# Two graph attention layers on one core: row sums, bias rows and a scatter of layer 0 in another place

## The chip, the cores and the metric

The kernel runs on one core of a Trainium2 chip. The metric is the device time of one execution in microseconds (us); less is better. The engines are named as in the profile: PE is TensorE, DVE is VectorE, ACT is ScalarE, POOL is GpSimd, SP is SyncE.

## The reference

Two layers of attention over a graph of 2708 nodes with 1024 features. Row i of the matrix `adj` holds ones at the neighbours of node i. Biases and weights are inputs; all is float32.

```
# layer 0
f = x @ Wf + bf ;  g = x @ Wg + bg
e = relu(f @ g.T)
attention = softmax(where(adj > 0, e, NEG), axis=1)
x = layernorm(x + attention @ (x @ W + bW))
# layer 1
h = x @ W1 ;  e = leaky_relu(h @ a1 + (h @ a2).T, 0.2)
attention = softmax(where(adj > 0, e, NEG), axis=1)
x = layernorm(x + relu(attention @ h))
```

`layernorm` takes mean and variance over the 1024 features of a row.

## The kernel before, in words

**Stages.** A node has few neighbours (at most 40), so the kernel never forms the 2708 x 2708 scores. It first reads `adj`, finds each row's neighbours as lists, and multiplies weights together (`M` = Wf times the transpose of Wg), so that a score is a dot product of `x M` of one node, plus a constant row, with the raw `x` of a neighbour. Then comes layer 0, block after block, and then layer 1. A last part (`general_path`) runs only for inputs whose lists don't fit, which is not the case here.

**Blocks and tiles.** Nodes are sorted by the number of neighbours and cut into groups of 32; four groups make a block of 128 nodes, and there are 22 blocks, one of them a small one. For a group, neighbours are gathered as tiles of 128 rows: 32 nodes times four neighbours. A group with up to 4t neighbours has t tiles, and a block of layer 0 some 20. The tiles of the gathered `x` rows live in `ring`, which has 20 places, so one block's tiles fill it. `u.tiles` puts the tiles of groups 0 and 1 first, by t, and then those of groups 2 and 3; gathers are issued in that order (line 635).

**A turn of layer 0's loop** (its body is around line 1039), for block `b`, the one before it (`back`) and the one after (`nxt`):

1. `sums` (line 703) multiplies the softmax weights `u.st` (128x32 for each tile) with the tiles in `ring` and adds them in the PSUM tile `po`. A tile has two matmuls, one for each half of the 1024 features. TensorE's columns are used as four column tiles of 32, told by `place`: column tile c takes group c in the first half of the features and group (c + 2) mod 4 in the second. Four matmuls, one for each column tile, make a step.
2. When both halves of a tile are done, its place in `ring` is free, and `gathers` (line 660) issues the gathers of the next block into free places, on POOL's queue.
3. The row sums of the softmax, `u.rs`, are added over the partitions by small matmuls with `stack` into a PSUM tile `pt`; their reciprocal `ri` scales `po` when ACT copies it to `y`.
4. TensorE turns the next blocks' `x` (`x_turn`), multiplies the sums of the block before with `W` (`product` with the bias bW), the `x` of a later block with `M` (`f_product`, with the constant row), and turns `y` for the next turn of the loop.
5. ACT spreads `x M` over 128 partitions (`Fr`), DVE takes the dots of it with the gathered tiles (`dots`), and the softmax (`soft`) makes the next block's `u.st`, and last its `u.rs` (line 701).
6. `close(back)` (line 919) is a generator: it adds the residual `z` and takes the layernorm's statistics; then ACT scales `z` and SP stores it to `X1S`; then DVE takes two dots that layer 1 needs, into further columns of `z`; last, POOL scatters `z` to the table `T1` in DRAM, which layer 1 gathers from. It is begun at the end of a turn of the loop (line 1080) and continued in the next one. `z` is a single buffer, `zs`, for all blocks but the last two; `load_residual` (line 913) fills it by a gather on POOL's queue.

**Bias rows.** A bias row of float32 values is held as three rows of bfloat16 that add up to it: `rows3[0:3]` for the constant row of `x M`, `rows3[32:35]` for bW. A matmul of `ones3` (three rows of ones) with them begins each product's accumulation (lines 546 and 566).

**What sets the order.** Each engine runs its instructions in program order: `InOrder` (line 61) pins it, and Tile puts in the semaphores that the data needs. So the order of calls in the loop is the order in each engine's queue. On POOL, after the tile gathers of `sums`, the turn of the loop issues `load_x` (`xb`, a later block's own rows), `load_residual` (`z`), and four list gathers of `load_lists` (`SL`). The PSUM pools `ps_t` and `ps_m` have two buffers each, `ps_s` (for `po`) has one.

Of the kernel before, what the change touches and what calls it, by code (L numbers as in the profile page):

```python
# [8 lines left out]
F32 = mybir.dt.float32  # L9
BF16 = mybir.dt.bfloat16  # L10
# [96 lines left out]
def listed_path(ctx, tc, x, adj, Wf, bf, Wg, bg, W, bW, W1, a1, a2, out):  # L107

    nc = tc.nc
    P = 128  # L110
# [36 lines left out]
    make_identity(nc, ident)  # L147
    ones = const.tile([P, 1], F32, name="ones")
    nc.gpsimd.memset(ones, 1.0)
    ones3 = const.tile([35, P], BF16, name="ones3")  # L150
    nc.gpsimd.memset(ones3, 1.0)

    stack = const.tile([P, 32], F32, name="stack")
    rep = const.tile([P, Q, 32], F32, name="rep")
# [16 lines left out]
    f1 = const.tile([P, NB], F32, name="f1")  # L171
    nc.gpsimd.memset(f1, 0.0)
    s0 = const.tile([P, 1], F32, name="s0")
    rows3 = const.tile([35, D], BF16, name="rows3")
    c3, b3 = rows3[0:3], rows3[32:35]
    scores = [const.tile([P, Q, QT], F32, name=f"scores{i}") for i in range(2)]
    for t in scores:
# [357 lines left out]
    def product(n, xT, w, row=None):  # L535


        pm = ps_m.tile([P, H, 512], F32, name="pm")
        for h in range(H):
            half_product(pm, h, n, xT, w, row)  # L540
        return pm

    def half_product(pm, h, n, xT, w, row=None):
        c = slice(h * 512, (h + 1) * 512)
        if row is not None:
            pe.matmul(pm[:n, h, :], ones3[row:row + 3, :n], rows3[row:row + 3, c], start=True, stop=False)
        for k in range(KC):
            pe.matmul(pm[:n, h, :], xT[:, k, :n], w[:, k, c],
                      start=(row is None and k == 0), stop=(k == KC - 1))

    def two_products(n, xT, w, row=None):

        halves = [ps_m.tile([P, H, 512], F32, name="pm") for h in range(H)]
        for h in range(H):
            half_product(halves[h], h, n, xT, w, row)
        return halves

    def split_product(xT, w, parts, row=None, pm=None):

        pm = ps_m.tile([P, H, 512], F32, name="pm") if pm is None else pm
        for h in range(H):
            c = slice(h * 512, (h + 1) * 512)
            if row is not None:
                pe.matmul(pm[:32, h, :], ones3[row:row + 3, :32], rows3[row:row + 3, c], start=True, stop=False)
            for k in range(KC // Q):
                for p in range(Q):
                    i = p * KC // Q + k
                    pe.matmul(pm[32 * p:32 * p + 32, h, :], xT[:, i, :32], w[:, i, c],  # L570
                              start=(k == 0 and (row is None or p > 0)), stop=(k + 1 == KC // Q))
        yield
        act.copy(parts, flat(pm))
        yield
        pm = ps_m.tile([P, H, 512], F32, name="pm")
        for h in range(H):
            pe.matmul(pm[:, h, :], rep, parts[:, h * 512:(h + 1) * 512], start=True, stop=True)
        return pm
# [63 lines left out]
    class Layer:  # L642
# [57 lines left out]
            u.rs = small.tile([P, Q], F32, name="rs")  # L700
            dve.tensor_reduce(u.rs[:, :u.G], sc, AX.X, ALU.add)

        def sums(self, u, po, hooks, y):

            pt = ps_t.tile([P, 4, P], F32, name="pt")
            place = lambda k, h: 32 * ((k + 2 * h) % 4)
            for h in range(H):  # L710
                for k in range(u.G):
                    j = place(k, h)
                    pe.matmul(pt[j:j + 32, 0, h:h + 1], stack, u.rs[:, k:k + 1], start=True, stop=True)
            ri = small.tile([P, H], F32, name="ri")
            spans = [(slice(0, P), slice(0, H))] if u.G == 4 else \
                [(slice(j, j + 32), slice(h, h + 1)) for h in range(H) for j in (place(0, h),)]
            for rows, h in spans:
                dve.reciprocal(ri[rows, h], pt[rows, 0, h])
            index = {(k, t): m for m, (k, g, t) in enumerate(u.tiles)}

            queues = []
            for c in range(4):
                two = [(k, h) for h, k in enumerate((c, (c + 2) % 4)) if k < u.G]
                queues.append([(k, h, t) for t in range(u.T) for k, h in two if t < TILES[u.gs[k]]])
            done, halves = 0, {}
            while any(queues):
                now = [q.pop(0) for q in queues if q]
                for k, h, t in now:
                    j = place(k, h)
                    pe.matmul(po[j:j + 32, h, :], u.st[:, u.col[k, t], :],  # L730
                              self.rows(u.at + index[k, t])[:, h * 512:(h + 1) * 512],
                              start=(t == 0), stop=(t == TILES[u.gs[k]] - 1))
                for k, h, t in now:
                    halves[k, t] = halves.get((k, t), 0) + 1
                    if halves[k, t] == H:
                        self.free.add(u.at + index[k, t])
                        self.gathers()
                        for f in hooks.get(done, []):
                            f()
                        done += 1  # L740
            for k, fs in sorted(hooks.items()):
                if k >= done:
                    for f in fs:
                        f()
            for h in range(H):
                rows = slice(0, P) if u.G == 4 else slice(place(0, h), place(0, h) + 32)
                c = slice(h * 512, (h + 1) * 512)
                act.activation(y[rows, c], po[rows, h, :], AF.Copy, scale=ri[rows, h:h + 1])
# [107 lines left out]
    with ExitStack() as s0s:  # L856
# [155 lines left out]
        for k, u in enumerate(units):  # L1012
            nxt = units[k + 1] if k + 1 < len(units) else None
            b = u.b
            back = seq[k - 1] if k > 0 else None
            ahead = seq[k + 2] if k + 2 < NB else None

            first = k == 0
            po = ps_s.tile([P, H, 512], F32, name="po")
            y[b] = yp.tile([P, D], F32, name="y")  # L1020
            if back is not None:
                for _ in yTs[back][1]:
                    pass
            reps = list(range(len(nxt.gs))) if nxt is not None and not first else []
            for r in reps[:1]:
                replicate(nxt.b, r)
            next(closing, None)
            if loaded is not None:
                q_dot(loaded)
                loaded = None  # L1030
            next(closing, None)
            for r in reps[1:3]:
                replicate(nxt.b, r)
            if nxt is None:

                for _ in closing:
                    pass
                Wp[back] = product(P, yTs.pop(back)[0], Wt, 32)
            lay.sums(u, po, {12: [lambda s=closing: [None for _ in s]]}, y[b])
            closing = iter(())  # L1040
            if ahead is not None and not first:
                x_turn(ahead)
            if k + 3 < NB and not first:
                loaded = seq[k + 3]
                load_x(loaded)
            if back is not None and nxt is not None:
                load_residual(back)
                if back > 0:
                    Wp[back] = product(P, yTs.pop(back)[0], Wt, 32)
                else:  # L1050
                    Wp[back] = whole(split_product(yTs.pop(back)[0], Wt, frp.tile([P, D], F32, name="Fr"), 32))
            if k + 2 == NB:
                load_residual(b)
            spreading = iter(())
            if ahead is not None and not first:
                spreading = q_spread(ahead)
                next(spreading)
            for r in reps[3:]:
                replicate(nxt.b, r)
            if ahead is not None and not first:  # L1060
                f_product(ahead)
            if ahead == NB - 1:
                sp.dma_start(M, W1.rearrange("(k p) d -> p k d", p=P))
            yT = tp.tile([P, KC, P], F32, name="xT")
            steps = turn(y[b], nrows[b], yT, halves=True)
            next(steps)
            yTs[b] = yT, steps
            if k + 2 == NB:
                for _ in steps:
                    pass  # L1070
            if k + 4 < NB and not first:
                load_lists(seq[k + 4])
            if nxt is not None:
                dots(nxt, 0, len(nxt.tiles))
            for _ in spreading:
                pass
            if nxt is not None:
                soft(nxt)
            if back is not None:
                closing = close(back)  # L1080
                next(closing)
        b = NB - 1
        load_residual(b)
        for _ in yTs[b][1]:
            pass
        Wp[b] = two_products(P, yTs.pop(b)[0], Wt, 32)
        for _ in closing:
            pass
        for _ in close(b):
# [521 lines left out]
```

## Time and profile before

| | us |
|---|---|
| median of 3 runs | 1772.31 |
| lowest, highest | 1768.69, 1783.73 |
| the profiled execution | 1778.06 |
| its span | 1776.3 |
| gathers of `ring` from `x`: 405 on POOL, busy | 438.6 |
| dots of layer 0: 402 on DVE, busy | 494.4 |
| matmuls into `po` from `ring`, both layers: 2616, busy | 322.7 |
| bias matmuls into `pm`: 86, busy | 33.7 |
| idle of PE ahead of the row sums (340 small matmuls) | 27.3 |

The lists and the weights take the first 276 us of the span, layer 0's loop the time to 1172 us, with a start of its first sums at 276.86 us, and layer 1 the rest. Each engine's instructions are shown with the idle time ahead of them and what ended it. Busy times of one engine don't add up to a bound: an engine can be busy in one stage and wait in another, and what counts is the wait that ends last in each turn of the loop.

### The profile page before, as it was taken

Reading aid. Unit: us, or ns where it says so; the run is one execution under the profiler, and the core shown is the slowest. Engines: PE = TensorE matmul, PEld = TensorE weight load, DVE = VectorE, ACT = ScalarE, POOL = GpSimd, SP = SyncE. Lnnn points to the kernel's source line nnn. Section 1 sums busy time; section 2 is a strip of 40 time slices with the busy share of each in tenths; the row PEclk is TensorE's granted clock in tenths of the full one; section 3 lists DMA queues with packets and bytes.
Section 4 is the critical chain, followed back from the end, with each engine's and each line's share of the span. In section 5 each row is a group of like instructions: output and inputs, shape, how many; then the busy total and the mean of one; then the engine's idle time right before and its main releaser. Section 6 shows DMA issues by size and latency. Waiting matters only on the chain. (4 is left out here: it accounts for less than half of the span.)

```text
span 1776.3 us, 22882 instructions
## 1 busy us (share of the span) xinstructions
PE 1586.4 (89%) x6969; PEld 677.2 (38%) x6969; DVE 1295.3 (73%) x4262; ACT 643.4 (36%) x902; POOL 1188.0 (67%) x1192
## 2 busy tenths in 40 slices
PE   5999389899999999999999999739899897998896
PEld 3444133343444443443444444313344333343342
DVE  5879756888888888888888887637656556665652
ACT  4545454444444455454555554101111111111111
POOL 8878476467666666667666664167777777777740
PEclk9999789899999999999999999969999999999998
DMA  7646168568777777777787787299999999999960
GB/s 284 245 160 240 44 227 318 207 213 289 291 283 270 264 250 256 272 282 266 277 295 278 268 296 297 88 359 368 365 369 394 392 392 378 383 395 391 391 250 37
DMA packets 149984, 502.79 MB, mean 283 GB/s; under 512 B 32340, under 2 KB 32372, under 8 KB 147144
## 3 DMA queue, kind: packets, MB, share of 16 engines
q0 software_dynamic: 132032, 428.29, 65.3%
q1 hardware_dynamic: 10202, 55.72, 8.4%
q10 hardware_dynamic: 7618, 17.23, 2.7%
q8 instruction: 57, 0.93, 0.2%
q14 instruction: 75, 0.61, 0.1%
HBM read 509.64 MB, written 33.75 MB: 306 GB/s over the span
## 5 line engine op out<-in xcount | busy, mean ns | idle before, releaser
L71 POOL DMA_INDIRECT ring<-in_x_dram,SL x405 | 438.6, 1083 | 253.1 <-issue 91.4
L71 DVE SCALAR_TENSOR_TENSOR j<-ring,Fr 128x1024 bf16<-128x1024 f32 x402 | 494.4, 1230 | 82.5 <-DMA ring<-in_x_dram,SL 55.7
L71 PE MATMUL po<-ring,st 128*32 128x512 f32 x2616 | 322.7, 618 | 47.8 <-ACT y L71 30.4
L71 ACT COPY Fr<-pm 32x1024 f32<-32x1024 f32 (+2 forms) x353 | 340.7, 965 | 21.1 <-PE pm L71 16.4
L71 PE MATMUL pm<-M,yT 128*128 128x512 f32 (+1 forms) x704 | 313.3, 598 | 0.5 <-ACT yT L71 0.5
L71 PE MATMUL pm<-M,xT 128*128 128x512 f32 x672 | 307.2, 611 | 0.0
L71 PE MATMUL pm<-Wt,xT 128*128 128x512 f32 (+1 forms) x704 | 303.5, 599 | 0.0
L71 POOL DMA_INDIRECT ring<-T,SL x249 | 246.9, 992 | 83.3 <-issue 69.9
L71 ACT ACTIVATE scores<-scores 128x12 f32<-128x12 f32 (+9 forms) x65 | 14.0, 216 | 669.3 <-DVE scores L71 669.3
L71 PEld LDWEIGHTS pm<-M,yT 128*128 128x128 f32 (+1 forms) x704 | 127.8, 186 | 184.7 <-issue 183.5
L71 PEld LDWEIGHTS pm<-M,xT 128*128 128x128 f32 x672 | 127.1, 194 | 165.3 <-issue 165.3
L71 PEld LDWEIGHTS po<-ring,st 128*32 128x32 f32 x2616 | 103.8, 114 | 222.9 <-issue 182.3
L71 POOL DMA_INDIRECT more<-T,SL x156 | 154.7, 992 | 47.5 <-issue 40.7
L71 PEld LDWEIGHTS pm<-Wt,xT 128*128 128x128 f32 (+1 forms) x704 | 125.0, 186 | 151.8 <-issue 151.1
L409 POOL TENSOR_TENSOR adj<-adj,iota 128x2708 f32<-128x2708 f32 (+3 forms) x23 | 130.5, 5685 | 24.4 <-ACT adj L71 24.3
L412 DVE MAX8 cand<-adj 128x8 f32<-128x136 f32 (+2 forms) x440 | 97.2, 285 | 35.8 <-POOL adj L409 35.8
L71 PE MATMUL pm<-halfT,WfT 128*128 128x512 f32 x256 | 113.2, 597 | 1.1 <-ACT WfT L71 1.1
L71 POOL DMA_INDIRECT SL<-LD,idq x85 | 86.0, 1011 | 25.8 <-issue 22.4
L71 PE MATMUL po<-more,st 128*32 128x512 f32 x624 | 83.8, 632 | 17.8 <-ACT y L71 17.8
L71 DVE TENSOR_SCALAR scores<-ring,f1q 128x4 f32<-128x4 f32 (+6 forms) x69 | 16.0, 238 | 99.3 <-DMA ring<-T,SL 95.9
L71 PEld LDWEIGHTS pm<-halfT,WfT 128*128 128x128 f32 x256 | 48.0, 192 | 57.4 <-issue 54.7
L71 ACT ACTIVATE y<-po,ri 128x512 f32<-128x512 f32 (+1 forms) x88 | 57.5, 678 | 20.9 <-PE po L71 20.3
(211 smaller groups left out, 1509.0 us busy)
## 6 DMA issues: line engine op xcount, KB each, us to landing
adj<-in_adj_dram SPq DMA_DIRECT2D x21, 1354.0 KB
X1S<-z SPq DMA_DIRECT2D x19, 512.0 KB
ring<-in_x_dram,SL POOLq DMA_INDIRECT x405, 6.6
rows<-in_L_gnn_Wg_dram ACTq DMA_DIRECT2D x8, 512.0 KB
rows<-in_L_gnn_Wf_dram ACTq DMA_DIRECT2D x8, 512.0 KB
rows<-in_L_gnn_W_dram ACTq DMA_DIRECT2D x8, 512.0 KB
Wt<-in_L_gnn_W_dram ACTq DMA_DIRECT2D x1, 4096.0 KB
M<-in_L_gnn_W_dram SPq DMA_DIRECT2D x1, 4096.0 KB
```

Source lines behind the costliest of these rows:

```text
L71: made = self.tc.keep_in_program_order(op(*args, **kwargs))
L409: nc.gpsimd.tensor_tensor(k[:n, cut], k[:n, cut], iota[:n, cut], op=ALU.mult)
L412: nc.vector.max(cand[:n, s, :], k[:n, s * SEG:min((s + 1) * SEG, N)])
```

## The change

In `sums`, the row sums' small matmuls move from ahead of the first tile's matmuls to behind the step after which four tiles (or `u.T`, if less) are done; the reciprocal is emitted behind the last tile's matmuls. Column tiles 2 and 3 begin with the second half of the features instead of the first. The hook that ran the rest of `close(back)`, its scatter, when 12 tiles were done is gone: the loop runs that rest when `sums` has returned, with all its gathers issued. `ones3` becomes `pick`, 128 rows with two columns, one for each bias; `rows3` has 128 rows, zero but for the two times three; the bias matmul contracts over all 128 rows. In `product` and `two_products` both halves' bias matmuls now come ahead of both halves' other matmuls.

```diff
-    ones3 = const.tile([35, P], BF16, name="ones3")
-    nc.gpsimd.memset(ones3, 1.0)
+    pick = const.tile([P, 2], BF16, name="pick")
+    nc.gpsimd.memset(pick, 0.0)
+    nc.gpsimd.memset(pick[0:3, 0:1], 1.0)
+    nc.gpsimd.memset(pick[32:35, 1:2], 1.0)
...
-    rows3 = const.tile([35, D], BF16, name="rows3")
+    rows3 = const.tile([P, D], BF16, name="rows3")
+    nc.gpsimd.memset(rows3, 0.0)
...
         for h in range(H):
+            bias_row(pm, h, n, row)
+        for h in range(H):
             half_product(pm, h, n, xT, w, row)
...
+    def bias_row(pm, h, n, row):
+        pe.matmul(pm[:n, h, :], pick[:, row:row + 1].to_broadcast([P, n]), rows3[:, h * 512:(h + 1) * 512], start=True, stop=False)
+
     def half_product(pm, h, n, xT, w, row=None):
         c = slice(h * 512, (h + 1) * 512)
-        if row is not None:
-            pe.matmul(pm[:n, h, :], ones3[row:row + 3, :n], rows3[row:row + 3, c], start=True, stop=False)
...
-        def sums(self, u, po, hooks, y):
+        def sums(self, u, po, y):
...
-            pt = ps_t.tile([P, 4, P], F32, name="pt")
             place = lambda k, h: 32 * ((k + 2 * h) % 4)
-            for h in range(H):
-                for k in range(u.G):
-                    j = place(k, h)
-                    pe.matmul(pt[j:j + 32, 0, h:h + 1], stack, u.rs[:, k:k + 1], start=True, stop=True)
-            ri = small.tile([P, H], F32, name="ri")
...
+            def totals():
+                pt = ps_t.tile([P, 4, P], F32, name="pt")
+                for h in range(H):
+                    for k in range(u.G):
+                        j = place(k, h)
+                        pe.matmul(pt[j:j + 32, 0, h:h + 1], stack, u.rs[:, k:k + 1], start=True, stop=True)
+                return pt
...
                 two = [(k, h) for h, k in enumerate((c, (c + 2) % 4)) if k < u.G]
+                if c > 1:
+                    two.reverse()
...
             while any(queues):
+                if pt is None and done >= min(4, u.T):
+                    pt = totals()
...
                         self.gathers()
-                        for f in hooks.get(done, []):
-                            f()
                         done += 1
...
+            if pt is None:
+                pt = totals()
+            ri = small.tile([P, H], F32, name="ri")
...
-            lay.sums(u, po, {12: [lambda s=closing: [None for _ in s]]}, y[b])
+            lay.sums(u, po, y[b])
+            for _ in closing:
+                pass
```

The bias matmul of `split_product` changes in the same way, and the calls pass the column 1 of `pick` instead of the row 32.

More of the change, by code (lines that the diff above doesn't have):

```diff
@@ L553, in two_products @@
         halves = [ps_m.tile([P, H, 512], F32, name="pm") for h in range(H)]
+        if row is not None:
+            for h in range(H):
+                bias_row(halves[h], h, n, row)
         for h in range(H):
@@ L565, in split_product @@
             if row is not None:
-                pe.matmul(pm[:32, h, :], ones3[row:row + 3, :32], rows3[row:row + 3, c], start=True, stop=False)
+                pe.matmul(pm[:32, h, :], pick[:, row:row + 1].to_broadcast([P, 32]), rows3[:, c], start=True, stop=False)
             for k in range(KC // Q):
@@ L701, in soft @@
             dve.tensor_reduce(u.rs[:, :u.G], sc, AX.X, ALU.add)
-        def sums(self, u, po, hooks, y):
-            pt = ps_t.tile([P, 4, P], F32, name="pt")
+        def sums(self, u, po, y):
             place = lambda k, h: 32 * ((k + 2 * h) % 4)
-            for h in range(H):
-                for k in range(u.G):
-                    j = place(k, h)
-                    pe.matmul(pt[j:j + 32, 0, h:h + 1], stack, u.rs[:, k:k + 1], start=True, stop=True)
-            ri = small.tile([P, H], F32, name="ri")
[L715 to L718, printed above, removed]
+            def totals():
+                pt = ps_t.tile([P, 4, P], F32, name="pt")
+                for h in range(H):
+                    for k in range(u.G):
+                        j = place(k, h)
+                        pe.matmul(pt[j:j + 32, 0, h:h + 1], stack, u.rs[:, k:k + 1], start=True, stop=True)
+                return pt
             index = {(k, t): m for m, (k, g, t) in enumerate(u.tiles)}
@@ L723, in sums @@
                 two = [(k, h) for h, k in enumerate((c, (c + 2) % 4)) if k < u.G]
+                if c > 1:
+                    two.reverse()
                 queues.append([(k, h, t) for t in range(u.T) for k, h in two if t < TILES[u.gs[k]]])
-            done, halves = 0, {}
+            done, halves, pt = 0, {}, None
             while any(queues):
+                if pt is None and done >= min(4, u.T):
+                    pt = totals()
                 now = [q.pop(0) for q in queues if q]
@@ L737, in sums @@
                         self.gathers()
-                        for f in hooks.get(done, []):
-                            f()
                         done += 1
[L741 to L744, printed above, removed]
+            if pt is None:
+                pt = totals()
+            ri = small.tile([P, H], F32, name="ri")
+            spans = [(slice(0, P), slice(0, H))] if u.G == 4 else \
+                [(slice(j, j + 32), slice(h, h + 1)) for h in range(H) for j in (place(0, h),)]
+            for rows, h in spans:
+                dve.reciprocal(ri[rows, h], pt[rows, 0, h])
             for h in range(H):
@@ L1037, in listed_path @@
                     pass
-                Wp[back] = product(P, yTs.pop(back)[0], Wt, 32)
-            lay.sums(u, po, {12: [lambda s=closing: [None for _ in s]]}, y[b])
+                Wp[back] = product(P, yTs.pop(back)[0], Wt, 1)
+            lay.sums(u, po, y[b])
+            for _ in closing:
+                pass
             closing = iter(())
@@ L1048, in listed_path @@
                 if back > 0:
-                    Wp[back] = product(P, yTs.pop(back)[0], Wt, 32)
+                    Wp[back] = product(P, yTs.pop(back)[0], Wt, 1)
                 else:
-                    Wp[back] = whole(split_product(yTs.pop(back)[0], Wt, frp.tile([P, D], F32, name="Fr"), 32))
+                    Wp[back] = whole(split_product(yTs.pop(back)[0], Wt, frp.tile([P, D], F32, name="Fr"), 1))
             if k + 2 == NB:
@@ L1085, in listed_path @@
             pass
-        Wp[b] = two_products(P, yTs.pop(b)[0], Wt, 32)
+        Wp[b] = two_products(P, yTs.pop(b)[0], Wt, 1)
         for _ in closing:
```

## The prediction

> **What bounds the kernel now.** I first read the busy times of the engines.
>
> ```profile
> PE 1586.4 (89%) x6969; PEld 677.2 (38%) x6969; DVE 1295.3 (73%) x4262; ACT 643.4 (36%) x902; POOL 1188.0 (67%) x1192
> ```
>
> TensorE looks like the bound, but that is an average over three stages. All that changes lies in layer 0 (276 to 1172 us of the span), so I went on to its timeline, engine by engine. From the sums that start at 369.33 us to those at 1043.80 us lie 16 nearly equal periods: 674.5 / 16 = **42.15 us a block**. I took the block at 960 us. Rows are start, duration, engine, line, operation, and in brackets the idle time before it with what ended it. On TensorE:
>
> ```profile
> 960.78 0.29 PE L71 MATMUL pt<-rs,stack 128*32 128x1 f32 x14 [0.88 <-DVE rs L71]
> ...
> 960.94 8.76 PE L71 MATMUL po<-ring,st 128*32 128x512 f32 x79
> 969.63 1.36 PE L71 MATMUL pt<-ident,xb 128*128 128x128 f32 x8
> 970.93 0.38 PE L71 MATMUL pm<-rows,ones 3*128 3x512 bf16 x1
> 971.24 7.13 PE L71 MATMUL pm<-Wt,xT 128*128 128x512 f32 x16
> ...
> 1000.48 1.04 PE L71 MATMUL pt<-ident,y 128*128 128x128 f32 x8
> 1002.64 0.29 PE L71 MATMUL pt<-rs,stack 128*32 128x1 f32 x14 [1.13 <-DVE rs L71]
> ```
>
> The reader is to see that TensorE has no gap inside the block, but waits before the row sums of the next one for VectorE's `rs`. Its own work is 1001.5 - 960.8 = 40.7 us, so it is close to the bound without being it. VectorE and POOL show who is late:
>
> ```profile
> 963.11 0.99 POOL L71 DMA_INDIRECT ring<-in_x_dram,SL  x1 [5.28 <-DVE bst L71]
> ...
> 971.39 1.01 POOL L71 DMA_INDIRECT T<-z,ids  x1 [0.30 <-issue]
> 972.71 1.34 POOL L71 DMA_INDIRECT ring<-in_x_dram,SL  x1 [0.30 <-issue]
> ...
> 992.18 0.99 POOL L71 DMA_INDIRECT xb<-in_x_dram,ids  x1 [0.30 <-issue]
> 993.48 0.99 POOL L71 DMA_INDIRECT z<-in_x_dram,ids  x1 [0.30 <-DVE j L71]
> ```
>
> ```profile
> 976.43 1.23 DVE L71 SCALAR_TENSOR_TENSOR j<-ring,Fr 128x1024 bf16<-128x1024 f32 x1 [0.75 <-DMA ring<-in_x_dram,SL]
> 978.15 1.23 DVE L71 SCALAR_TENSOR_TENSOR j<-ring,Fr 128x1024 bf16<-128x1024 f32 x1 [0.49 <-DMA ring<-in_x_dram,SL]
> 980.72 1.23 DVE L71 SCALAR_TENSOR_TENSOR j<-ring,Fr 128x1024 bf16<-128x1024 f32 x1 [1.34 <-DMA ring<-in_x_dram,SL]
> ```
>
> POOL issues one gather each 1.3 us (0.99 and 0.30), starting 2.2 us after the sums start in 15 of the 16 blocks whatever VectorE does (so `bst` as the releaser is a coincidence; TensorE frees the slot). VectorE's dots run at 1.27 us each, so once they have caught up with the stream they go at its pace. The longest wait, 1.34 us, is for the gather at 972.71, the first one behind the scatter at 971.39. So the loop is: sums free slots, POOL gathers, tiles land some 8 us later, dots, softmax, next sums; and the scatter stands in the middle of it.
>
> **What the Trainium skill says.** "DMA: Bandwidth & Descriptors", section "Anatomy of one DMA — SWDGE (gpsimd) path": a wait for a semaphore is served on the issuing sequencer before dispatch, and most of a small transfer's fixed cost is the receipt of its last write. The trace agrees: at the end of layer 0 a lone scatter starts on POOL at 1153.14, and the gather that depends on it starts at 1159.73, after 5.26 us idle in which POOL does nothing else. "TensorEngine Tiling (Array Packing)", section "Key Properties": a change of tiling mode drains the array. "TensorE: Matmul & The Clock Gate", section "Back-to-back issue gap", gives N/2.4 + 2.5 ns, 216 ns for 512 columns in bf16. The trace has 14.76 us for a product with two bias rows and 14.00 us for one of 32 matmuls without (1747.58), so a 3-row bias takes 0.38 us; that fits a drain on top of the 216 ns, but doesn't prove it.
>
> **Part 1, row sums and reciprocal.** The sums of a block now need `st`, not `rs`. In the timeline `st` ends 0.36 us before the sums start; with the 0.14 us that TensorE takes to see it, the sums start 0.2 us earlier, and where an ACT copy of `xT` held the row sums' PSUM buffer (12.8 us in all in the group) more. The 16 small matmuls (0.13 us) go behind the first eight large ones: no work saved, but off the start. The reciprocal keeps its place among VectorE's instructions (behind the two dots of the layernorm, ahead of the next block's), nine us later than TensorE has the totals: cost nothing; without that cover, 0.16 us.
>
> **Part 2, column tiles 2 and 3 begin with the other half.** The first tile's second half is the third matmul instead of the seventh: four steps of 0.11 us, so the first gather may start 0.44 us earlier. With part 1 the stream starts 0.7 us earlier after `st`. The number of matmuls and of columns stays. Bounds: 0 to 0.7 us a block, and nothing if POOL isn't free by then.
>
> **Part 3, bias rows.** 84 full and 4 small ones go from 3 to 128 contracted rows. At 0.22 us instead of 0.38 that is 0.3 us for each product, 0.6 us a block on TensorE: its work goes to some 40.2 us, with the start of the row sums in it. Bounds: -0.7 (both cost only 216 ns and no drain elsewhere) to +0.2 us a block (a full weight load that isn't hidden, 0.19 us from the 128x128 loads, shown for f32 only). It counts only where TensorE is the bound: the last two periods of the loop and the last product. Setup: three small memsets (0.1 us each) and one of 128x1024 in bf16 (0.5 to 1 us, from 0.49 us for 128x484 f32) on POOL, which idles 2.02 us ahead of its first adjacency tile: hidden, else +1 us.
>
> **Part 4, the scatter.** Of the layernorm's generator only its last step is left for the hook to run, and for the buffer `z` that step issues this scatter alone. Removed from the stream: one POOL issue of 1.3 us ahead of the last 14 gathers, so the last tiles land 1.3 + 0.7 = 2.0 us earlier. VectorE's waits in the block (2.6 us) shrink to some 0.6 us; its own work, 9.7 us from `st` to the first dot, 25.5 us of dots and 3.9 us of softmax, is 39.1 us. Added: the scatter reads the only `z` buffer, and the residual's gather writes it. Before, 22 us lay between the two on POOL; now one issue (`xb`). So the `z` gather **must wait on POOL for the scatter to land**, and behind it in that queue stand four list gathers and then the next block's 20 tile gathers; SP's queue is not touched, its store of `z` is issued before as now. Lone, scatter start to dependent start is 6.6 us (1153.14 to 1159.73); behind a busy stream I take 6.8 us. Lower end 6.0, upper 9.0 (the median landing of the scatters in mid-stream, 8.2 us, and 0.8 us to wake). Without the wait `z` would start 2.6 us after the scatter, so 4.2 us are added. POOL's round is then 27 issues of 1.3 us (35.0), 1.8 us of slow issues (mean over the 16 blocks of the last gather's start less the first's less 26.0), and 4.2: **41.0 us**. That is more than TensorE's 40.2 to 40.5 and VectorE's 39.1, and becomes the bound. VectorE sees nearly the same limit from the other side: `z` lands 4.4 us after its gather starts (a near idle DMA: 4.3 for `xb` at 992), about 1 us after the softmax is done, so the add and all behind it, the dots too, start 1 us late: 40.1 us and the rest of the waits.
>
> **The sum.** 16 periods x (42.15 - 41.0) = 18.4 us. The two short periods after them, where TensorE has no wait over 0.9 us, 0.6 us each: 1.2. The period ahead of them (325 to 369 us, no scatter's wait yet), 0.5; the last product, 0.3. Together 20 us. The profiled execution took 1778.06 us (span 1776.3 and 1.76 around it), so 1758 there; it lies 5.75 above the median of the three runs shown, so against that median, 1772.31, I say **1752**.
>
> **Rivals.** *TensorE becomes the bound.* If the `z` gather starts within 6 us of the scatter, POOL's round is under 40.3 and TensorE's work decides: 40.3 us, 16 x 1.85 + 2 = 32, so 1740. For it: the `xb` gather near the end of the stream lands in 4.3 us. Against: the lone scatter already took 6.6 us to its dependent.
>
> *The wait for the scatter takes more than was removed (slower).* It decides from 7.9 us between the scatter's start and the `z` gather's: 36.8 + 7.9 - 2.6 = 42.1. At 9.0 us the round is 43.2 us, 16 x 1.05 - 2 = +15, so 1787. For it: the mid-stream landing of 8.2 us. Against: behind the scatter only one gather follows instead of 14, and a tile gather late in the stream (906.13) lands in 5.9 us.
>
> *The move does nothing.* In mid-block the DMA engines are busy for their whole time (share about 1.0 from 888 to 914 us, some 400 GB/s), and slow issues could grow by what the scatter leaves: then only the 0.7 us of parts 1 and 2 less a little is left, 16 x 0.4 = 6, so 1766. Against: the scatter's bytes leave the stream as well.
>
> **How the numbers follow.** Chances: the forecast 0.50 (1744 to 1762 with the landing half a us either way), TensorE 0.17, slower 0.20, nothing 0.13. The range 1737 to 1788 takes in TensorE's floor and the 9.0 us wait; the likeliest case's own is 1744 to 1762. One per cent, about what a measurement here can tell from no change, is 17.7 us: faster needs under 1754.6. That holds for 0.6 of the forecast and all of TensorE's case, and a little of the last: 0.50. Slower, over 1790, takes the upper part of the slower case and what I have not thought of: 0.13. Within: 0.37.
>
> **What would show it.** Right: on POOL a scatter directly behind the last tile gather, `xb`, then a `z` gather with some 4 us idle ahead released by the DMA of `T<-z`; the dots' waits near the seventh tile gone; the first gather less than 2.2 us after the sums start, or with no idle ahead; bias matmuls 0.22 us apart from their successor. Wrong: a `z` gather with 0.30 us ahead of it (no wait at all), or over 8 us after the scatter; products of 14.76 us still (part 3); or TensorE idle for `rs` or `st` as long as now.

## The result, and the profile after

| | before | after |
|---|---|---|
| median, us | 1773.95 (4 runs) | 1750.05 (4 runs) |
| lowest to highest, us | 1768.69 to 1783.73 | 1746.39 to 1750.47 |
| profiled execution, its span, us | 1778.06, 1776.3 | 1750.29, 1748.6 |
| mean of the 16 like periods of layer 0, us | 42.15 | 40.55 |

The ratio is 0.9841, with a 95% interval of 0.9813 to 0.9869: faster by 1.6%. (On two of the three chips used below some executions are slow ones, up to 5% longer at a lower granted clock; the ratios leave these out and the medians beside them don't, so the two need not agree.) Of the 27.7 us between the spans, the 16 periods give 25.7 (674.47 less 648.77). Ahead of them the first sums' tile matmuls start 1.5 earlier, the first turn of the loop is 2.7 longer and the second 2.8 shorter; behind them the two short periods are 1.7 longer, the last turn 0.6 shorter, and layer 1 is 1.5 shorter.

TensorE in the block at 896 us of the changed kernel (columns as before: start, duration, engine, line, operation, idle time ahead and what ended it):

```profile
905.60 0.66 PE L71 MATMUL pt<-ident,xb 128*128 128x128 f32 x4 [0.53 <-DVE ri L71]
906.09 0.59 PE L71 MATMUL pm<-rows,pick 128*128 128x512 bf16 x2
906.52 13.90 PE L71 MATMUL pm<-Wt,xT 128*128 128x512 f32 x32
920.26 0.28 PE L71 MATMUL pt<-qd,rep 128*128 128x4 f32 x2
...
936.58 1.92 PE L71 MATMUL po<-ring,st 128*32 128x512 f32 x16 [0.98 <-DVE st L71]
938.32 0.28 PE L71 MATMUL pt<-rs,stack 128*32 128x1 f32 x16
```

Three things are to be seen. The sums now wait for `st` and begin with tiles; the row sums come behind them without a wait. A product with its two bias rows takes 920.26 - 906.09 = 14.17 us from the first bias row to the instruction behind the product. And there is a new wait, for `ri`, ahead of the second half of the `xb` transposes. In the kernel before, the same product took 1027.44 - 1012.77 = 14.67 us:

```profile
1012.77 0.38 PE L71 MATMUL pm<-rows,ones 3*128 3x512 bf16 x1
1013.09 7.13 PE L71 MATMUL pm<-Wt,xT 128*128 128x512 f32 x16
1020.16 0.39 PE L71 MATMUL pm<-rows,ones 3*128 3x512 bf16 x1
1020.47 7.13 PE L71 MATMUL pm<-Wt,xT 128*128 128x512 f32 x16
1027.44 0.28 PE L71 MATMUL pt<-qd,rep 128*128 128x4 f32 x2
```

POOL in the same stretch, and VectorE's addition of the residual:

```profile
926.13 1.01 POOL L71 DMA_INDIRECT T<-z,ids  x1 [0.30 <-issue]
927.45 1.02 POOL L71 DMA_INDIRECT xb<-in_x_dram,ids  x1 [0.30 <-issue]
931.64 1.75 POOL L71 DMA_INDIRECT z<-in_x_dram,ids  x1 [3.16 <-DVE j L71]
933.69 1.00 POOL L71 DMA_INDIRECT SL<-LD,idq  x1 [0.30 <-issue]
...
937.69 1.00 POOL L71 DMA_INDIRECT SL<-LD,idq  x1 [0.30 <-issue]
939.00 1.00 POOL L71 DMA_INDIRECT ring<-in_x_dram,SL  x1 [0.30 <-PE pt L71]
```

```profile
936.77 1.23 DVE L71 TENSOR_TENSOR z<-pm,z 128x1024 f32<-128x1024 f32 x1 [0.17 <-DMA z<-in_x_dram,ids]
```

The scatter now stands behind the stream. The `z` gather has 3.16 us of idle time ahead of it (VectorE's `j` is a coincidence: that dot had nothing to do with `z`; what it waits for is the scatter's landing). The next block's first tile gather follows the fourth list gather with 0.30 us between them, so POOL has no more room. And `z` lands just too late for VectorE. Over 18 blocks the `z` gather starts 6.8 us after the scatter on average (4.2 to 8.7).

Two of VectorE's waits in the 16 periods, first of the kernel before, then of the changed one (engine, what waited, for whom, us in total, times, longest):

```profile
DVE j L71 <- DMA ring<-in_x_dram,SL: 49.5, 61, 1.8
...
DVE z L71 <- DMA z<-in_x_dram,ids: 2.0, 1, 2.0
```

```profile
DVE j L71 <- DMA ring<-in_x_dram,SL: 11.7, 21, 1.2
...
DVE z L71 <- DMA z<-in_x_dram,ids: 4.9, 11, 1.3
```

The dots' wait for gathered tiles fell by 37.8 us, 2.4 us a block, of which 1.6 became time. So far it looks as the prediction had it. The experiments say that the same gain comes without part 4.

### The profile page after: what moved, and what is told of

Same layout as the page of the kernel before. It is cut to its first block, busy times and chain, and to the rows that moved or that the text cites. A ratio compares the mean times of both kernels' runs of the same rounds, so it can differ in the third digit from the quotient of the medians.

```text
span 1748.6 us, 23112 instructions
## 1 busy us (share of the span) xinstructions
PE 1563.6 (89%) x6969; PEld 675.5 (39%) x6969; DVE 1297.5 (74%) x4262; ACT 643.5 (37%) x902; POOL 1180.9 (68%) x1195
## 5 line engine op out<-in xcount | busy, mean ns | idle before, releaser
L71 POOL DMA_INDIRECT ring<-in_x_dram,SL x405 | 429.9, 1062 | 164.0 <-issue 70.0
L71 DVE SCALAR_TENSOR_TENSOR j<-ring,Fr 128x1024 bf16<-128x1024 f32 x402 | 493.9, 1229 | 41.1 <-DMA ring<-in_x_dram,SL 13.9
L71 PE MATMUL pm<-M,xT 128*128 128x512 f32 x672 | 297.5, 601 | 0.0
L71 PEld LDWEIGHTS pm<-Wt,xT 128*128 128x128 f32 (+1 forms) x704 | 131.0, 189 | 163.4 <-issue 154.6
L71 PEld LDWEIGHTS po<-ring,st 128*32 128x32 f32 x2616 | 95.9, 113 | 229.8 <-issue 174.0
L71 POOL DMA_INDIRECT z<-in_x_dram,ids x21 | 24.0, 1142 | 87.1 <-DVE j L71 36.4
```

Of the source, the lines that this page charges most:

```text
L71: made = self.tc.keep_in_program_order(op(*args, **kwargs))
```

## The experiments

My theory was that the scatter's place in the stream of gathers was what the change mended, and that parts 1 to 3 were small or hidden. The rival was that these three had brought the gain. The first four kernels ran on one chip (kernel before: 1776.15 us, median of 20 runs).

**Part 4 alone** on the kernel before:

```diff
-            lay.sums(u, po, {12: [lambda s=closing: [None for _ in s]]}, y[b])
+            lay.sums(u, po, {}, y[b])
+            for _ in closing:
+                pass
```

> The kernel before with part 4 alone: the scatter behind the gathers, all else as before. Theory (the gather stream sets the block, and POOL's round with the wait for the scatter becomes the bound): VectorE's waits in the stream go, TensorE's own 40.7 us and the wait ahead of the residual's gather remain, so 41.2 us a block instead of 42.15, some 15 us faster, ratio to before 0.991. Rival (TensorE's shorter bias rows and earlier start brought the gain): ratio 1.00, with the wait for the scatter on POOL for nothing.

1765.58 us, ratio 0.9939 (0.9923 to 0.9954); periods of 41.5 us on average, median 41.1. The gain is real and two thirds of what I expected. In the profiled execution the 16 periods gave 10.4 us, and the first short period behind them took 7.4 back (47.2 us instead of 39.8, with VectorE waiting 7.7 us for the residual). What limits the 16 periods is to be seen on TensorE:

```profile
908.56 0.30 PE L71 MATMUL pt<-rs,stack 128*32 128x1 f32 x16 [0.29 <-ACT xT L71]
908.71 8.77 PE L71 MATMUL po<-ring,st 128*32 128x512 f32 x80
917.41 1.09 PE L71 MATMUL pt<-ident,xb 128*128 128x128 f32 x8
...
949.31 0.30 PE L71 MATMUL pt<-rs,stack 128*32 128x1 f32 x16 [0.29 <-ACT xT L71]
```

In this block TensorE waits for nothing but 0.29 us: of 949.31 - 908.56 = 40.75 us, 40.5 are its own work with the old bias rows. Other blocks are longer, where the residual is late or the stream slow.

**Part 4 undone** in the changed kernel, the hook put back at 12 tiles:

```diff
-        def sums(self, u, po, y):
+        def sums(self, u, po, hooks, y):
...
                         self.gathers()
+                        for f in hooks.get(done, []):
+                            f()
                         done += 1
...
-            lay.sums(u, po, y[b])
-            for _ in closing:
-                pass
+            lay.sums(u, po, {12: [lambda s=closing: [None for _ in s]]}, y[b])
```

> The changed kernel with part 4 alone undone: the scatter issued by the hook when 12 tiles are done. Theory: the stream starts about 1 us earlier after the softmax, but its last 14 gathers stand behind the scatter again, so about 41.1 us a block, ratio to before 0.990. Rival (parts 1 to 3 brought it): as the changed kernel, ratio 0.984. The residual's gather has no wait in either.

1745.73 us, ratio 0.9828 (0.9792 to 0.9863). **The rival was right**: parts 1 to 3 without the scatter's move are as fast as the whole change (0.9841, 0.9813 to 0.9869). The periods are 40.39 us. In its stream on POOL the first gather starts 1.35 us after the sums (893.55) instead of 2.19, and the scatter is in the middle as before:

```profile
894.90 1.00 POOL L71 DMA_INDIRECT ring<-in_x_dram,SL  x1 [4.13 <-DVE z L71]
...
903.02 0.99 POOL L71 DMA_INDIRECT ring<-in_x_dram,SL  x1 [0.30 <-issue]
904.31 1.01 POOL L71 DMA_INDIRECT T<-z,ids  x1 [0.30 <-issue]
905.63 1.18 POOL L71 DMA_INDIRECT ring<-in_x_dram,SL  x1 [0.30 <-issue]
```

```profile
913.41 1.22 DVE L71 SCALAR_TENSOR_TENSOR j<-ring,Fr 128x1024 bf16<-128x1024 f32 x1 [1.14 <-DMA ring<-in_x_dram,SL]
```

The dots wait once, 1.14 us, for the tile behind the scatter; in the kernel before it was 0.75, 0.49 and 1.34 us in the block shown. In all 16 periods this wait is 19.2 us, before 49.5: an earlier stream has enough of a lead for the scatter to pass through with less than half the wait.

**A second buffer for the residual** in the changed kernel. The constant vector `rb` gives the room, and its dot is taken with `u1b` instead, so layer 0's attention weights are others, with the same work:

```diff
-            dot(xb[b][:n], rb, n, qs[:n])
+            dot(xb[b][:n], u1b, n, qs[:n])
...
-            Z[b] = zs if b + 2 < NB else t[:, at, :]
+            Z[b] = (rb if b % 2 else zs) if b + 2 < NB else t[:, at, :]
```

> The changed kernel with a second buffer for the residual, so that its gather needn't wait for the scatter of the block before. To make room the constant of layer 0's scores is taken as the dot of x with another vector of the same size, so the attention weights of layer 0 are others; all work stays. Theory (the wait for the scatter is the new bound, through POOL's queue or through a late residual): the idle time of 3 to 4 us ahead of the residual's gather goes, and the block falls from 40.6 us to TensorE's 39.6 to 40.0, some 10 us faster than the changed kernel, ratio to before 0.978. Rival (TensorE is the bound already): no change against the changed kernel, 0.984.

1734.11 us, ratio 0.9762 (0.9727 to 0.9796), clear of the changed kernel's interval; periods of 39.74 us. The waits of TensorE in the 16 periods, with two buffers and then in the changed kernel:

```profile
PE po L71 <- DVE st L71: 2.4, 5, 0.6
PE pt L71 <- DVE ri L71: 2.0, 6, 0.6
```

```profile
PE pt L71 <- DVE ri L71: 10.5, 13, 2.0
PE po L71 <- DVE st L71: 5.4, 9, 1.0
```

So with the wait for the scatter gone TensorE is the bound, with 4.4 us of waits in 16 blocks, at 39.5 us of work. With the scatter in mid-stream a period took 40.39 us, with the scatter behind the gathers 40.55, and with a second buffer as well 39.74: the move can save about 0.65 us a block, and the single `z` takes 0.8 back. (Its sums also start 2.5 us earlier and its first turn is 3 us shorter than in the changed kernel, 48.0 against 51.1; I can't say that this comes of the second buffer.)

**The list gathers ahead of the residual's**, so that POOL works while the scatter lands:

```diff
+            if k + 4 < NB and not first:
+                load_lists(seq[k + 4])
             if back is not None and nxt is not None:
                 load_residual(back)
```

(and taken out at its old place behind the transposes of `y`)

> The changed kernel with the four list gathers issued ahead of the residual's gather instead of behind it, so that POOL does them while the scatter lands. If it is POOL's queue that the wait holds up: its round loses the 3 to 4 us of idle time, as with two buffers, ratio to before 0.978. If it is the late landing of the residual on VectorE: the residual's gather starts some 2 us later (7.8 us behind the scatter instead of 5.5), and the block is longer, 41.5 us or more, ratio 0.993.

1744.1 us, ratio 0.9814 (0.9769 to 0.9858), between the two cases. The `z` gather starts 7.9 us after the scatter in nearly every block, as expected, and VectorE's addition waits longer for it:

```profile
DVE z L71 <- DMA z<-in_x_dram,ids: 9.1, 12, 2.7
```

(380 to 1000 us.) But the tile gathers start 1.35 us after the sums in nearly all blocks again, and the median period is 40.1 us; three blocks near 900 to 1000 us took 41 to 44. This order trades POOL's idle time for a later residual. It fits the reading that both were at work in the changed kernel with neither far ahead, but the interval doesn't part it from the changed kernel, so that is not shown.

The next eight runs fell on two other chips, four on each, on which the kernel before took 1926 us (the first four) and 1955 us (the others). In the busiest slices of layer 1 DMA moves some 350 GB/s there where the first chip has 391. TensorE differs too: it pauses ahead of matmuls while the profile shows nothing that it waits for ("issue"), which it never does in the 16 periods of the two kernels in the tables above. From the run with parts 1 and 2 alone:

```profile
773.65 1.55 PE L71 MATMUL pm<-M,xT 128*128 128x512 f32 x3
776.41 0.59 PE L71 MATMUL pm<-M,xT 128*128 128x512 f32 x1 [1.21 <-issue]
778.52 0.59 PE L71 MATMUL pm<-M,xT 128*128 128x512 f32 x1 [1.52 <-issue]
780.62 1.01 PE L71 MATMUL pm<-M,xT 128*128 128x512 f32 x1 [1.50 <-issue]
```

Such a product takes some 26 us instead of 14.7, and its block 52 instead of 41.5. The cause of the pauses is open. The intervals are up to three times as wide as on the first chip, and a ratio can still shift by about 1% with the executions that are taken; so only ratios to the kernel before on the same chip are used, and differences under 1% are called open.

**Part 3 alone**, twice (with both bias rows ahead of both halves, as in the changed kernel):

```diff
-            pe.matmul(pm[:n, h, :], ones3[row:row + 3, :n], rows3[row:row + 3, c], start=True, stop=False)
+        pe.matmul(pm[:n, h, :], pick[:, row:row + 1].to_broadcast([P, n]), rows3[:, h * 512:(h + 1) * 512], start=True, stop=False)
```

> The kernel before with part 3 alone: bias rows over 128 rows, ahead of both halves. Theory (the gather stream, begun by the sums, sets the block; TensorE is next): TensorE's work falls by the 1.2 us a block that the changed kernel shows, but it waits for the softmax 1.2 us longer, so the block stays at 42.1 us, ratio to before 0.998 to 1.000. Rival (TensorE's own chain sets the block): 16 blocks and the ends, 20 us, ratio 0.989.

> Part 3 alone on the kernel before, as in the run on a chip with slower DMA, where it brought nothing (1.004). If the gather stream sets the block, nothing here either: TensorE waits 1.2 us longer for the softmax, ratio to before 0.998 to 1.002. If TensorE's chain counts: 0.989.

1915.99 us, ratio 1.0042 (0.9994 to 1.0090), and 1948.36 us, ratio 1.0018 (0.9953 to 1.0083): no gain that these runs can show, and not the rival's 0.989, though the products are as short as in the changed kernel (981.38 - 967.08 = 14.30 us, the two small matmuls between them taken in). Where the time went is on TensorE, in the first of the two:

```profile
955.61 0.29 PE L71 MATMUL pt<-rs,stack 128*32 128x1 f32 x14 [3.06 <-DVE rs L71]
...
967.08 0.59 PE L71 MATMUL pm<-rows,pick 128*128 128x512 bf16 x2
967.51 13.90 PE L71 MATMUL pm<-Wt,xT 128*128 128x512 f32 x32
981.38 0.59 PE L71 MATMUL pm<-rows,pick 128*128 128x512 bf16 x2
```

In this block the work saved has become a wait of 3.1 us for the softmax; in the 16 periods TensorE waits 21.6 us for `rs` in all.

**Parts 1 and 2 alone**, twice: the `sums` of the changed kernel with the hook, and the old bias rows.

> The kernel before with parts 1 and 2 alone: row sums within the sums, two column tiles begin with the other half; the scatter by its hook and the three bias rows as before. Theory: the stream of gathers starts about 1.1 us earlier after the softmax, until TensorE's 40.7 us of work and its waits hold it, so 41.1 us a block, ratio to before 0.991; with the shorter bias rows on top it would be the 40.4 us of the changed kernel with the hook. Rival (the start doesn't matter, since the dots wait in mid-stream): ratio 1.000.

> Parts 1 and 2 alone on the kernel before. The stream starts 1 us earlier, and TensorE with its old bias rows (40.7 us of work and some waits) becomes the bound: 41.1 to 41.4 us a block, ratio to before 0.989 to 0.991. Then parts 1 to 3 together (0.983) are more than 1 and 2 and 3 alone. If instead parts 1 and 2 bring all: 0.983.

1914.1 us, ratio 0.9899 (0.9812 to 0.9986), and 1921.56 us, ratio 0.9845 (0.9729 to 0.9962). Both intervals lie under 1 and hold 0.983 as well as 0.990. The first is doubtful all the same: the fastest of its 6 executions took 1891.05 us, and the fastest of the 27 of the kernel before 1883.55. That parts 1 to 3 are more than their sum is not shown. But part 3 does count on top of the other two: parts 1 to 3 took 40.39 us a period on the first chip, and with the old bias rows TensorE's own work alone is 40.5 us.

**Part 2 alone:**

```diff
+                if c > 1:
+                    two.reverse()
```

> The kernel before with part 2 alone: column tiles 2 and 3 begin with the other half. Theory: the first tile is free after the first step instead of the second, the first gather starts 1.75 us after the sums instead of 2.19, and the block is 0.4 us shorter: ratio to before 0.996. Rival: no change, 1.000.

1889.62 us, ratio 0.9821 (0.9767 to 0.9876): more than expected. The first gather starts 1.33 us after the sums:

```profile
602.92 1.47 PE L71 MATMUL po<-ring,st 128*32 128x512 f32 x12
```

```profile
604.25 1.00 POOL L71 DMA_INDIRECT ring<-in_x_dram,SL  x1 [5.62 <-PE po L71]
```

So two lines bring the whole of what the gathers start earlier behind the sums. How the gain in time is split between parts 1 and 2 is open: with both parts the ratios were 0.9899 and 0.9845, against 0.9821 here, but TensorE's pauses differ as much. With both parts, on the same chip, two blocks had a product of 26 us, and the sums took 8.85 us in 14 of the 16 blocks; with part 2 alone no product was so long, but the sums took over 10 us in 9 of the 16. Part 1 alone was not run.

**The list gathers split**, two ahead of the residual's and two behind it, and the changed kernel beside it:

```diff
+            split = k + 4 < NB and not first
+            if split:
+                load_lists(seq[k + 4], slice(0, 2))
             if back is not None and nxt is not None:
                 load_residual(back)
+                if split:
+                    load_lists(seq[k + 4], slice(2, 4))
```

> The changed kernel with two of the four list gathers ahead of the residual's gather and two behind it. If the wait for the scatter (5.5 us from its start) costs time only as idle time of POOL's queue, two issues of 1.3 us take up most of it without making the residual later than in the changed kernel: 39.8 us a block, as with two buffers, ratio to before 0.977. If it isn't POOL's idle time: as the changed kernel, 0.984.

> The changed kernel with two list gathers ahead of the residual's gather and two behind it, beside the changed kernel itself on the same chip. If POOL's idle time behind the scatter is what part 4 gave back: 39.9 us a block, some 10 us faster than the changed kernel (0.994 of it). If not: no difference.

> The changed kernel itself, as the measure for the three others on this chip: ratio to before 0.984.

0.9816 (0.9718 to 0.9914) and 0.9806 (0.9731 to 0.9881) with the split, 1901.13 and 1912.86 us; the changed kernel beside the second of them 0.9826 (0.9779 to 0.9873), 1904.49 us. The expected 0.6% was not found, and would be hidden in these intervals: open. The profiled executions don't settle it: the sums took 8.85 us in most blocks of the split and some 11 in nearly all of the changed kernel, while the split had the more of the long products. The changed kernel's own gain holds on this chip.

## Why the prediction was right, and where it wasn't

- **The time**, 1752 us, was 2 us off; direction and size were right, the nearness in part luck, since errors offset each other. The 16 periods took 40.55 us where I had 41.0 and gave 25.7 us where I had 18.4. Against that the two short periods behind them became 1.7 us longer instead of 1.2 shorter, and the median moved by 23.9 us where the profiled executions moved by 27.8. In the first short period VectorE waits 6.5 us for the residual and TensorE 3.1 us for `ri` behind it; the period took 42.5 us, and 38.6 with two buffers or with the scatter in mid-stream. So the price of the single `z` was forecast for the long periods and not for this one.
- **Part 4** went as described: the scatter behind the last tile gather, the `z` gather 6.8 us behind the scatter as forecast, POOL without room, the residual late by some tenths. What failed is its place in the sum, where it carried nearly all of the 18.4 us; the third rival put what would be left without it at 0.4 us a block, and parts 1 to 3 alone brought 42.15 - 40.39 = 1.76. So a right time came from a sum with the wrong part in front. Alone part 4 brings 0.6%. With parts 1 to 3 in place it brings nothing that these runs can measure (0.9828 without it, 0.9841 with it): what is left to save with the earlier stream, 0.65 us a block, is about what the single `z` costs, 0.8.
- **Part 2** was mis-sized: four steps of 0.11 us, 0.44 us, against 0.84 us measured (2.19 to 1.35, and 1.33 alone). I counted the starts of matmuls to the seventh and the third, and not what lies between a matmul of the second step and its release; which of that it is, the trace doesn't show, since matmuls' ends are modelled. The third rival's "only the 0.7 us of parts 1 and 2" came of the same term.
- **Part 3** was mis-sized: 0.3 us a product was forecast, 0.5 measured (14.67 to 14.17), 1.0 us a block. I priced a new bias row right, at 0.22 us, and an old one too low, at 0.38 from whole products. The 14.76 us of one with bias rows is misread: to the end of its last matmul it is 14.83 in nearly all (1012.77 to 1027.60). And the 14.00 us of one without came from layer 1; the same 32 matmuls take 13.90 here now. From start to start, the 32 behind the old rows took 14.03 us (14.67 less two times 0.32), and 13.74 now. That would fit what the Trainium skill says of a drain at each change of tiling mode ("TensorEngine Tiling (Array Packing)", section "Key Properties"), if a matmul of 3 rows is such a change. No run here shows it: the change also moved both bias rows ahead of both halves, and the two weren't tried apart. TensorE's floor is 39.5 us a block, not 40.2. That it counts only where TensorE is the bound was right: alone it brought nothing that can be measured, twice.
- **Part 1**: the reciprocal was costed at nothing, since TensorE has the totals long before. It wasn't: the reciprocal still comes behind the layernorm's dots on VectorE, and it holds `pt`, one of two buffers that the `xb` transposes need. The wait for `ri` ahead of those went from 0.6 to 13.7 us in all. Much of it comes with the late residual, whose layernorm stands ahead of the reciprocal: in the 16 periods it is 10.5 us in the changed kernel, 5.8 with part 4 undone and 2.0 with two buffers.
- Not foreseen: in the first turn TensorE now waits 4.7 us for `Wt`, which it starts to use at 295.3 us; before it had it at 291.9. The load is issued at 273.4 and 274.2 us. In the turn's first 15 us the DMA engines are full (share 1.0, 410 GB/s), and the tile gathers, which now begin 1.3 us after the first sums instead of 3.6, take part of that. This reading was not tried; the first turn is 51 us too in the run with part 4 undone, and 48.3 with part 4 alone, so on the first chip the longer turn is seen with parts 1 to 3 and not without them. But with two buffers it was 48.0 us again, though TensorE waited 4.2 us for `Wt` there too; so the wait alone doesn't account for it, and the cause is open.

## What to carry to other kernels

When a loop runs through several engines, ask how much lead each gain gives to the next step, not only what it removes: taking an issue out of the middle of a stream of gathers brought 0.6% alone, an earlier start of the stream with less work on TensorE 1.7%, and all together 1.6%, since both shorten the same wait and the single buffer takes its share back. An issue moved to the end of a queue is charged there for the buffer that it still holds; a second buffer was worth 0.8% where the move alone was worth nothing on top. To see what a bundle of edits is made of, undo the one you believe in: that told more than any of the parts alone.

## What the runs showed of the hardware

Two bf16 bias rows of 512 columns over 128 contracted rows take 0.43 us together (906.09 to 906.52), and the 32 matmuls behind them 0.43 us each; with 3 contracted rows one took 0.32 us (1012.77 to 1013.09) and the matmuls behind it 0.44 us each (16 in the 7.07 us from 1013.09 to 1020.16). So the rows of zeros cost nothing here. How much of the difference comes of the 128 rows, and how much of having the two bias rows next to each other, is not shown.
